# A four-layer graph network on one core: where a group's sums run, and when projections are issued

## The chip, the cores and the metric

The kernel runs on one core of a Trainium2 chip. The metric is the device time of one execution in microseconds (us); the time of a kernel is the median of its runs. Five engines with queues of their own work side by side: PE (matrix products; its weight loads are listed apart as PEld), DVE (vector), ACT (scalar functions), POOL, and SP, which here issues all large DMA transfers in the order of its queue.

## The reference, cut to what matters

There are N = 3327 nodes with D = 256 features, and a dense matrix `adj` of which about one per cent is not zero. Every layer normalizes, applies a ReLU and adds its result to x.

```python
# layer 0, two steps; R is adj + I with rows divided by their sums
for n in range(2):
    A = top_p_attention(Xa)          # softmax(q @ k.T); of each row, the largest
                                     # values that make up 0.9 of the sum are kept
    Xf = R @ Xf
    Xa = A @ Xa
    Z = Z + Xf @ U1[n].T + Xa @ U2[n].T
x = x + layernorm(h + Z)
# layer 1: weights tanh(adj * adj) where adj > 0
x = x + relu(new_adj @ (tanh(h @ W_proj + b_proj) @ W_gcn) + b_gcn)
# layers 2 and 3: graph attention over the places where adj > 0 (layer 2: or the diagonal)
Wh = h @ W
e = leaky_relu((Wh @ a[:256])[:, None] + (Wh @ a[256:])[None, :], 0.2)
x = x + softmax(where(mask, e, -9e15)) @ Wh      # layer 3: elu of this product
```

## The kernel before

The nodes are padded to 3328, 26 tiles of 128 rows. All products are in f32. The program is written tile by tile; a scheduler then orders the instructions of each engine when the kernel is built, so an engine's order is not quite that of the lines. During a run each engine goes through its own list in order.

**Layer 0.** In each of the two steps (s = 0 and 1) the rows are worked in groups of three tiles. For a group, scores are made (L1042) and moved from PSUM with a running maximum (L1016), exponentials are taken on ACT (L1025), and a threshold is sought for each row: a first guess (L1065 to L1104, with partial sums at L1085), and then four rounds (L1115 to L1158). A round sums, for each row, the values at or above the guess, and moves the guess. The sum of a tile is one pass on DVE (L1131), or two passes on ACT, a Relu and a Sign (L1126, written to `junk_a`), whose sums are put together on DVE (L1137, L1138). `ON_ACT = [2, 2, 1, 2]` says how many of a group's three tiles have their sums on ACT in each round. Before a round ACT negates the guess (`minus`, L1119); a round ends with a new guess (`v`, L1158). After the rounds the kept values are selected on DVE (L1173, L1176, L1187).

`weighted` then does a tile's attention product: transposes of the kept values (L951), their copy to `wt` on ACT (L953), 26 products (L941), the row `xa` (L963), a load of the tile's other row `xf_in` (L935), transposes of both (L785, copied at L786), and the product with U1 and U2 (L971).

`neighbours` makes one tile of R @ Xf: it loads the adjacency tile in four chunks `blk` (L906; three buffers), adds the diagonal on POOL (L913), runs 26 products into `ps_acc` (L915) and scales the row on ACT (`xf_row`, L923), which is written to memory (L924) and later read back as `xf_in`. In step 0 only, ACT also takes the sign of each chunk (`sg`, L909), and SP writes it out as int8 (`sign_d`, L910), to serve as the mask in layers 2 and 3. Groups overlap: a new one starts while the one before is in its products; during a group's rounds, `neighbours` of some tiles is laid beside it. The first group of a step has no earlier group's products beside it.

**Layer 1** is a loop over the 26 tiles (L1469 to L1500). Half a tile of `adj` is loaded (L1475), DVE multiplies (L1478), ACT takes the tanh (L1479), and PE runs 13 products (L1482) into `ps_wide`. Then `summed(it - 1)` adds bias and residual and takes statistics, and `entered2(it - 2)` prepares layer 2 for the tile two back: `Entry.tile_in` normalizes (`hr` on ACT, L1400), transposes (L785 on PE), copies to `ht` on ACT (L786), and projects on PE (L1405), with copies to `sd` and `wh` on ACT (L1409, L1410). After the last tile of each span of four, `spread` transposes and copies the column terms (L1422, L1425). The loop also loads rows of `adj` (L1494), from which DVE makes the mask `pos` (L1496).

**Layers 2 and 3** are `attention` over seven spans of four tiles: exponentials on ACT (L1585, L1586), their maximum and the mask on DVE (L1587, L1588), products on PE (L1594). While attention 2 runs, the finished tiles are prepared for layer 3 through the same `Entry`, in slots of a list `todo`. An `Entry` also makes, when it is created, a shift from its weights: a product on DVE, a matmul, a reduction and four small POOL steps (L1373 to L1385).

Of the kernel before, what the change touches and what calls it, by code (L numbers as in the profile page):

```python
# [20 lines left out]
P = 128  # L21
# [45 lines left out]
def kernel(  # L67
# [678 lines left out]
    def layers(fast):  # L746
# [54 lines left out]
        def layer0(wp, mp, ap_, tp, sp):  # L801
# [97 lines left out]
            def neighbours(s, it, xf):  # L899

                acc = ps_acc()
                w = XW if s == 0 else D
                for chunks in QB:
                    n = len(chunks)
                    blk = ap_.tile([P, 7, P], F32, tag="blk", name="blk")
                    nc.sync.dma_start(blk[:, :n, :], adj_t[it, :, chunks[0] : chunks[0] + n, :])  # L906
                    if s == 0:
                        sg = tp.tile([P, 7, P], I8, tag="sg", bufs=1, name="sg")
                        nc.scalar.activation(sg[:, :n, :], blk[:, :n, :], AF.Sign)  # L909
                        nc.sync.dma_start(sign_d[it, :, chunks[0] : chunks[0] + n, :], sg[:, :n, :])  # L910
                    if it in chunks:
                        j = it - chunks[0]
                        nc.gpsimd.tensor_tensor(blk[:, j, :], blk[:, j, :], ident, ALU.add)  # L913
                    for j, jc in enumerate(chunks):
                        nc.tensor.matmul(  # L915
                            acc[:, :w], blk[:, j, :], xf(jc)[:, :w], start=(jc == 0), stop=(jc == NT - 1)
                        )
                    yield
                yield
                if s == 0:  # L920
                    nc.vector.reciprocal(rr[:, it : it + 1], acc[:, D : D + 1])
                row = tp.tile([P, D], F32, tag="xf_row", name="xf_row")
                nc.scalar.mul(row, acc[:, :D], rr[:, it : it + 1])  # L923
                nc.sync.dma_start((xf_d, xf2_d)[s][it * P : (it + 1) * P, :], row)  # L924
                yield

            def weighted(s, it, e, norm, xa, xa_next, us):

                if s == 0:
                    base = h(it)[:, :D]  # L930
                else:
                    base = tp.tile([P, D], F32, tag="base", bufs=1, name="base_row")
                    nc.sync.dma_start(base, zz_d[it * P : (it + 1) * P, :])
                xf_in = tp.tile([P, D], F32, tag="xf_in", name="xf_in")
                nc.sync.dma_start(xf_in, (xf_d, xf2_d)[s][it * P : (it + 1) * P, :])  # L935
                po = ps_out0()[:, :D]

                def products(wt, j0, m):
                    for k in range(m):
                        jc = j0 + k  # L940
                        nc.tensor.matmul(  # L941
                            po, wt[:, k * P : (k + 1) * P], xa(jc)[:, :D], start=(jc == 0), stop=(jc == NT - 1)
                        )

                ready = None
                for j0 in range(0, NT, 8):
                    m = min(8, NT - j0)
                    pt = ps_wide()
                    for k in range(m):
                        jc = j0 + k  # L950
                        nc.tensor.transpose(pt[:, k * P : (k + 1) * P], e[:, jc * P : (jc + 1) * P], ident)  # L951
                    wt = tp.tile([P, 8 * P], F32, tag="wt", name="wt")
                    nc.scalar.copy(wt[:, : m * P], pt[:, : m * P])  # L953
                    if ready:
                        products(*ready)
                    ready = wt, j0, m
                    yield
                products(*ready)
                if s == 0:
                    row = xa_next(it)[:, :D]  # L960
                else:
                    row = tp.tile([P, D], F32, tag="xa_row", bufs=1, name="xa_row")
                nc.scalar.mul(row, po, norm)  # L963
                yield
                xt = turned(row, "xt", 2)
                xft = turned(xf_in, "xft", 2)
                yield
                pz = ps_row()
                for n, (lhs, u) in enumerate(((xft, us[0]), (xt, us[1]))):
                    for cc in range(2):  # L970
                        nc.tensor.matmul(  # L971
                            pz[:, :D], lhs[:, cc, :], u[:, cc, :],
                            start=(n == 0 and cc == 0), stop=(n == 1 and cc == 1),
                        )
                if s == 0:
                    keys_of(xt, 1, it)
                yield
                zrow = tp.tile([P, D], F32, tag="zrow", bufs=1, name="zrow")
                nc.vector.tensor_tensor(zrow, pz[:, :D], base, ALU.add)
                nc.sync.dma_start(zz_d[it * P : (it + 1) * P, :], zrow)  # L980
                if s == 1:
                    norm_of(zrow, sp, "mv_z", mv_z[:, it, :])
                yield
                if s == 0:

                    xb = tp.tile([P, D], F32, tag="xa_row", bufs=1, name="xb")
                    r = rows_of(it)
                    for a, b in rows_to_load(it):
                        nc.sync.dma_start(xb[a:b], x[it * P + a : it * P + b])
                    nc.gpsimd.tensor_tensor(xb[:r], xb[:r], b_b[:r], ALU.add)  # L990
                    nc.sync.dma_start(xb_d[it * P : it * P + r, :], xb[:r])
# [9 lines left out]
            def group(s, tiles, xa, xf, xa_next, us, slots, products_of, also):  # L1001
# [111 lines left out]
                todo = list(products_of)  # L1113
                first = 2 if g == len(todo) else 0
                for r in range(ROUNDS):  # L1115
                    on_act = list(range(max(g - ON_ACT[r], g - 2 if g > 2 else 1), g)) if g > 1 else []
                    A = slice(on_act[0], g) if on_act else None
                    if on_act:
                        nc.scalar.mul(minus[:, 0, A], v[:, 3, A], -1.0)  # L1119
# [239 lines left out]
        class Entry:  # L1359
# [3 lines left out]


            def __init__(self, name, w, wh, dk_tag, eye):
                self.w, self.wh, self.eye, self.mv = w, wh, eye, {}
                for t in wh.halves:
                    nc.gpsimd.memset(t[:, :, D : D + 1], 1.0)
                self.sd = late.tile([P, NT, 2], F32, name=f"sd{name}")
                self.d2 = late.tile([P, NT], F32, name=f"d2{name}")  # L1370
                self.dk = slot(dk_tag, [P, NP], f"dk{name}")
                self.tops = late.tile([P, 4, len(spans)], F32, name=f"tops{name}")
                sq = late.tile([P, 2], F32, tag="sq", name="sq")  # L1373
                nc.vector.tensor_tensor(sq, w[:, :, D + 1], w[:, :, D + 1], ALU.mult)
                ps = ps_row()
                nc.tensor.matmul(ps[:, :2], ones, sq, start=True, stop=True)
                self.shift = late.tile([P, 1], F32, name=f"shift{name}")
                self.low = late.tile([P, 1], F32, name=f"low{name}")
                shift = self.shift
                nc.vector.tensor_reduce(shift, ps[:, :2], AX.X, ALU.add)  # L1380
                nc.gpsimd.tensor_scalar(shift, shift, 1.01 * D, EPS, ALU.mult, ALU.add)
# [1 line left out]
                nc.gpsimd.tensor_scalar(shift, shift, 1.0, None, ALU.add)  # L1383

                nc.gpsimd.tensor_scalar(self.low, shift, -1.0 + 2.0**-20, None, ALU.mult)  # L1385
                if not eye:

                    self.part = late.tile([P, D + 1], F32, name="part")
                    nc.gpsimd.memset(self.part, 0.0)

            def stats(self, it, src):

# [1 line left out]
                nc.gpsimd.tensor_scalar(mv[:, 0:1], mv[:, 0:1], mv[:, 1:2], -1.0, ALU.mult, ALU.mult)  # L1394
                self.mv[it] = mv

            def tile_in(self, it, src):
                hr = late.tile([P, D], F32, tag="hr", bufs=2, name="hr")
                mv = self.mv.pop(it)
                nc.scalar.activation(hr, src, AF.Relu, bias=mv[:, 0:1], scale=mv[:, 1:2])  # L1400
                ht = late.tile([P, D], F32, tag="ht", bufs=2, name="ht")
                transposed(hr, ht)
                ps = ps_row()
                for c in range(2):
                    nc.tensor.matmul(  # L1405
# [47 lines left out]
        with tc.tile_pool(name="l1", bufs=2, reuse_waits="tile") as l1:  # L1453
# [7 lines left out]
                nc.vector.scalar_tensor_tensor(xn(it), pre, 0.0, xs(it), ALU.max, ALU.add)  # L1461
                entry2.stats(it, xn(it))

            def entered2(it):
                entry2.tile_in(it, xn(it))
                if it in ends:
                    entry2.spread(ends.index(it))

            for it in range(NT):  # L1469
# [15 lines left out]
                if it >= 1:  # L1485
                    summed(it - 1)
                if it >= 2:
                    entered2(it - 2)
                ar = slot(f"e{it % 2}", [P, NP], "adj_rows")
                r = rows_of(it)  # L1490
                if r < P:
# [7 lines left out]
                nc.gpsimd.memset(pos[:, N:], 0)  # L1499
                nc.sync.dma_start(pos_d[it], pos)  # L1500
            summed(NT - 1)
            entered2(NT - 2)
            entered2(NT - 1)


        att = fast.enter_context(tc.tile_pool(name="att", bufs=1, reuse_waits="tile"))
# [9 lines left out]
        def attention(entry, finish, following=None):  # L1516
# [33 lines left out]
            for i, span in enumerate(spans):  # L1550
# [16 lines left out]
                for b, j0 in enumerate(range(0, NT, JB)):  # L1567
# [30 lines left out]
                    if 1 <= b <= len(ahead):  # L1598
# [5 lines left out]
                        )  # L1604
                        if b == len(ahead):
                            sb_next = scores_of(ahead, top)
                    if b and todo:
                        for work in todo.pop(0):
                            work()
# [10 lines left out]
                if following is not None:  # L1620

                    stats = [lambda it=it: following.stats(it, xn(it)) for it in span]
                    rest = [lambda it=it: following.tile_in(it, xn(it)) for it in span]
                    todo += [stats[:2]] + [rest[k : k + 1] + stats[k + 2 : k + 3] for k in range(n)]
                    todo.append([lambda i=i: following.spread(i)])
            for works in todo:
                for work in works:
                    work()
# [106 lines left out]
```

## Time and profile before

| what | value |
|---|---|
| median of 3 runs | 3104.74 us (3103.69 to 3111.75) |
| the profiled execution | 3100.91 us, its span 3099.1 us |
| mean granted PE clock in it | 0.973 of full speed |
| step 0: first group's guess is made (L1104) | at 106.6 us |
| step 0: its rounds end (L1158) | at 132.8, 150.2, 160.1, 177.3 us |
| step 0: first L951 of groups 0 to 3 | at 197.2, 290.8, 386.5, 479.0 us |
| step 1: first group's guess, rounds' ends | at 1056.6; 1074.6, 1090.5, 1099.7, 1115.1 us |
| layer 1 | about 1999 to 2371 us |
| attention 2, attention 3 | about 2371 to 2765, and to the end |

A line of the costliest groups names a line, an engine, an operation and output <- inputs; then the number of instructions, their busy time and the mean ns of one, and the idle time of the engine just ahead of them with what ended most of it. A line of the waits says which instruction waited for which, how many us in all, how often, and the longest. A line of the timeline gives start and length of an instruction, and in brackets the idle time before it.

### The profile page before, as it was taken

The page shows a single profiled execution, that of the slowest core. Times are in us where ns is not written, and L with a number is a line of the kernel's source. Part 1 is how long each engine was busy: PE and PEld are TensorE (multiplying, and loading weights), DVE is VectorE, ACT ScalarE, POOL GpSimd, SP SyncE. Part 2 cuts the span into 40 slices and gives each one's busy share as a digit, 9 for nine tenths or more (in the row PEclk, how much of TensorE's full clock was granted, in tenths as well). Part 3 has the DMA queues.
Part 4 walks back from the last instruction along what each step waited for, and adds up shares of the span by engine and source line. Part 5 has one row for each costly group of instructions (what it writes and reads, how often), then busy time and mean ns, then how long its engine had stood idle before and what let it go on. Part 6 is the DMA issues. An engine that isn't in the chain of part 4 may idle for free.

```text
span 3099.1 us, 37681 instructions
## 1 busy us (share of the span) xinstructions
PE 2823.0 (91%) x13454; PEld 2277.8 (73%) x13454; DVE 2370.4 (76%) x4133; ACT 1979.7 (64%) x2633; POOL 417.8 (13%) x742
## 2 busy tenths in 40 slices
PE   7788899999999899999999988999997999979998
PEld 5466677777778576667777767888886887758887
DVE  3678889778874588889876858377765999769996
ACT  6767787768773566687666555433334777657776
POOL 0120010000001001111110024211110333210000
PEclk9889999999999999999999989999998999989999
DMA  4431112321242231211232231388871211112221
GB/s 138 131 102 45 55 45 76 95 78 57 75 121 87 73 103 53 64 35 54 74 90 72 83 114 60 105 321 318 324 243 32 71 59 59 30 48 78 75 74 37
DMA packets 183035, 298.83 MB, mean 96 GB/s; under 512 B 24701, under 2 KB 137016, under 8 KB 179512
## 3 DMA queue, kind: packets, MB, share of 16 engines
q1 hardware_dynamic: 182838, 296.34, 30.3%
q8 instruction: 108, 1.77, 0.3%
q14 instruction: 89, 0.72, 0.1%
HBM read 251.97 MB, written 44.30 MB: 96 GB/s over the span
## 4 chain that ended last, share of the span: by engine, by line
DVE 38%; PE 27%; ACT 16%; issue 8%; DMA 7%; POOL 3%; SPq 0%; ACTq 0%; POOLq 0%; DVEq 0%
ACT junk_a L1126 9%; PE ps_wide L1594 5%; DVE below L1173 4%; PE ps_out L941 4%; PE ps_acc L915 4%; DVE w L1176 4%; PE ps_wide L1482 4%; DVE below L1131 3%; DVE e L1187 3%; DVE places L1601 3%; DVE places L1587 2%; DVE below L1085 2%; DVE places L1588 2%; DMA blk<-in_adj_t 2%; DMA adj_rows<-in_adj 2%
## 5 line engine op out<-in xcount | busy, mean ns | idle before, releaser
L1126 ACT ACTIVATE junk_a<-e,minus 128x3328 int8<-128x3328 f32 x208 | 638.8, 3071 | 3.7
L1594 PE MATMUL ps_wide<-wh,places 128*128 128x257 f32 x1872 | 451.2, 383 | 35.6 <-DVE places L1588 32.7
L1594 PEld LDWEIGHTS ps_wide<-wh,places 128*128 128x128 f32 x1872 | 353.3, 191 | 93.6 <-ACT places L1586 16.5
L915 PE MATMUL ps_acc<-h,blk 128*128 128x258 f32 x1352 | 333.3, 399 | 46.8 <-ACT xf_row L923 37.1
L915 PEld LDWEIGHTS ps_acc<-h,blk 128*128 128x128 f32 x1352 | 261.8, 198 | 102.3 <-ACT xf_row L923 42.7
L1016 DVE TENSOR_SCALAR_CACHE_REDUCE e<-ps_wide 128x1024 f32<-128x1024 f32 (+1 forms) x176 | 178.6, 1019 | 206.9 <-PE ps_wide L1042 206.4
L915 PE MATMUL ps_acc<-xf,blk 128*128 128x256 f32 x1352 | 312.9, 384 | 14.3 <-ACT xf_row L923 14.2
L941 PE MATMUL ps_out<-h,wt 128*128 128x256 f32 x1352 | 311.2, 381 | 4.7 <-ACT wt L953 4.7
L941 PE MATMUL ps_out<-xa,wt 128*128 128x256 f32 x1352 | 311.9, 381 | 0.9 <-ACT wt L953 0.7
L1585 ACT ACTIVATE places<-places,sd 128x512 f32<-128x512 f32 (+1 forms) x364 | 246.3, 684 | 100.5 <-PE ps_wide L1594 67.6
L1482 PE MATMUL ps_wide<-gw,blk 128*128 128x256 f32 x1352 | 300.9, 379 | 1.3 <-ACT blk L1479 1.3
L915 PEld LDWEIGHTS ps_acc<-xf,blk 128*128 128x128 f32 x1352 | 253.9, 191 | 61.8 <-ACT xf_row L923 19.3
L1482 PEld LDWEIGHTS ps_wide<-gw,blk 128*128 128x128 f32 x1352 | 254.5, 190 | 35.0 <-ACT blk L1479 1.7
L941 PEld LDWEIGHTS ps_out<-h,wt 128*128 128x128 f32 x1352 | 249.8, 190 | 40.1 <-ACT wt L953 6.3
L941 PEld LDWEIGHTS ps_out<-xa,wt 128*128 128x128 f32 x1352 | 249.4, 190 | 34.8 <-ACT wt L953 3.0
L1586 ACT ACTIVATE places<-places,d 128x512 f32<-128x512 f32 (+1 forms) x364 | 235.8, 682 | 48.7 <-DVE places L1587 48.2
L1131 DVE SCALAR_TENSOR_TENSOR below<-e,v 128x3328 f32<-128x3328 f32 x72 | 265.3, 3684 | 1.8
L1587 DVE TENSOR_TENSOR places<-places,places 128x1024 f32<-128x1024 f32 (+1 forms) x182 | 210.2, 1163 | 65.8 <-ACT places L1585 63.7
L1042 PE MATMUL ps_wide<-keys,q 64*128 64x512 f32 (+1 forms) x832 | 215.9, 570 | 17.8 <-DVE e L1016 14.8
L953 ACT COPY wt<-ps_wide 128x1024 f32<-128x1024 f32 x208 | 175.2, 846 | 86.2 <-PE ps_wide L951 85.6
L1588 DVE SCALAR_TENSOR_TENSOR places<-blk_s,places 128x1024 f32<-128x1024 int8 (+1 forms) x182 | 206.3, 1142 | 2.0
L1176 DVE MAX8 w<-below 128x8 f32<-128x3328 f32 x52 | 188.3, 3621 | 0.3
(275 smaller groups left out, 4312.6 us busy)
## 6 DMA issues: line engine op xcount, KB each, us to landing
blk<-in_adj_t SPq DMA_DIRECT2D x104, 448.0 KB, 3.5
blk<-in_adj_t SPq DMA_DIRECT2D x52, 832.0 KB, 7.1
adj_rows<-in_adj SPq DMA_DIRECT2D x25, 1663.5 KB, 8.4
blk<-in_adj_t SPq DMA_DIRECT2D x104, 384.0 KB, 3.3
blk_s<-sign_d SPq DMA_DIRECT2D x72, 256.0 KB, 2.9
blk_s<-pos_d SPq DMA_DIRECT2D x44, 416.0 KB, 3.6
pos_d<-pos SPq DMA_DIRECT2D x22, 416.0 KB, 2.9
xf_d<-xf_row SPq DMA_DIRECT2D x52, 128.0 KB, 2.4
```

The lines of the kernel that those rows point to most:

```text
L915: nc.tensor.matmul(acc[:, :w], blk[:, j, :], xf(jc)[:, :w], start=(jc == 0), stop=(jc == NT - 1))
L941: nc.tensor.matmul(po, wt[:, k * P : (k + 1) * P], xa(jc)[:, :D], start=(jc == 0), stop=(jc == NT - 1))
L1042: nc.tensor.matmul(pl[:, f * 512 : f * 512 + cw], q[f * DA : (f + 1) * DA, :], kt[f * DA : (f + 1) * DA, s, c0 : c0 + cw], start=True, sto ...
L1126: nc.scalar.activation(junk, es[i], (AF.Relu, AF.Sign)[n], bias=minus[:, 0, i : i + 1], accum_out=(ga, sa)[n][:, 0, i : i + 1],)
L1131: nc.vector.scalar_tensor_tensor(below, es[i], v[:, 3, i : i + 1], es[i], ALU.is_ge, ALU.mult, accum_out=v[:, 1, i : i + 1],)
L1176: nc.vector.max(w9[:, i, 1:9], below)
L1482: nc.tensor.matmul(po, filt[:, j * P : (j + 1) * P], gw(jc), start=(jc == 0), stop=(jc == NT - 1))
L1585: nc.scalar.activation(e1[:, :, q, :], s0, AF.Exp, bias=sd[:, jc + q, 1:2])
L1586: nc.scalar.activation(e2[:, :, q, :], s1, AF.Exp, bias=d2[:, jc + q : jc + q + 1])
L1587: nc.vector.tensor_tensor(e1, e1, e2, ALU.max)
L1588: nc.vector.scalar_tensor_tensor(e1, signs[:, :n, j : j + 2, :], 0.0, e1, ALU.is_gt, ALU.min)
L1594: nc.tensor.matmul(pos_[k], e1[:, k, q, :], wh(jc + q)[:, : D + 1], start=(jc + q == 0), stop=(eye and jc + q == NT - 1),)
```

## The change

It has four parts.

- In `neighbours`, `sg` gets the pool's two buffers in place of one; in `weighted`, `xf_in` gets one in place of two.
- In the rounds, the group that holds tile 0 has `most = 1`, so only its last tile has its sums on ACT in every round; all others keep `ON_ACT`. This is the first group of step 0 and of step 1.
- `tile_in` is split into `turned` (normalize, transposes, copy to `ht`) and `projected` (products, copies). In layer 1's loop, pass `it` does `turned(it - 2)` and `projected(it - 3)`; in attention 2's list, a slot has `turned` of one tile and `projected` of the tile before.
- The shift is made by a function `shifted`, called in the loop's pass 2 for layer 2, and in the second span of attention 2 for layer 3, rather than when the `Entry` is created.

```diff
-                        sg = tp.tile([P, 7, P], I8, tag="sg", bufs=1, name="sg")
+                        sg = tp.tile([P, 7, P], I8, tag="sg", name="sg")
...
-                xf_in = tp.tile([P, D], F32, tag="xf_in", name="xf_in")
+                xf_in = tp.tile([P, D], F32, tag="xf_in", bufs=1, name="xf_in")
...
-                    on_act = list(range(max(g - ON_ACT[r], g - 2 if g > 2 else 1), g)) if g > 1 else []
+
+                    most = 1 if tiles[0] == 0 else ON_ACT[r]
+                    on_act = list(range(max(g - most, g - 2 if g > 2 else 1), g)) if g > 1 else []
...
-            def tile_in(self, it, src):
+            def turned(self, it, src):
                 hr = late.tile([P, D], F32, tag="hr", bufs=2, name="hr")
                 mv = self.mv.pop(it)
                 nc.scalar.activation(hr, src, AF.Relu, bias=mv[:, 0:1], scale=mv[:, 1:2])
-                ht = late.tile([P, D], F32, tag="ht", bufs=2, name="ht")
-                transposed(hr, ht)
+                self.ht[it] = late.tile([P, D], F32, tag="ht", bufs=2, name="ht")
+                transposed(hr, self.ht[it])
+
+            def projected(self, it):
+                ht = self.ht.pop(it)
                 ps = ps_row()
...
                 if it >= 2:
-                    entered2(it - 2)
+                    entry2.turned(it - 2, xn(it - 2))
+                if it == 2:
+                    entry2.shifted()
+                if it >= 3:
+                    projected(it - 3)
...
             summed(NT - 1)
-            entered2(NT - 2)
-            entered2(NT - 1)
+            projected(NT - 3)
+            entry2.turned(NT - 2, xn(NT - 2))
+            projected(NT - 2)
+            entry2.turned(NT - 1, xn(NT - 1))
+            projected(NT - 1)
...
+                    if following is not None and (i, b) == (1, 1):
+                        following.shifted()
...
-                    rest = [lambda it=it: following.tile_in(it, xn(it)) for it in span]
-                    todo += [stats[:2]] + [rest[k : k + 1] + stats[k + 2 : k + 3] for k in range(n)]
-                    todo.append([lambda i=i: following.spread(i)])
+                    turned = [lambda it=it: following.turned(it, xn(it)) for it in span]
+                    made = [lambda it=it: following.projected(it) for it in span]
+                    todo += [stats[:2]] + [
+                        turned[k : k + 1] + made[max(k - 1, 0) : k] + stats[k + 2 : k + 3] for k in range(n)
+                    ]
+                    todo.append(made[-1:] + [lambda i=i: following.spread(i)])
```

The rest of the diff moves the shift's lines unchanged from `__init__` into `shifted`.

More of the change, by code (lines that the diff above doesn't have):

```diff
@@ L1365, in __init__ @@
             def __init__(self, name, w, wh, dk_tag, eye):
-                self.w, self.wh, self.eye, self.mv = w, wh, eye, {}
+                self.w, self.wh, self.eye, self.mv, self.ht = w, wh, eye, {}, {}
                 for t in wh.halves:
@@ L1372, in __init__, with shifted @@
                 self.tops = late.tile([P, 4, len(spans)], F32, name=f"tops{name}")
+                self.shift = late.tile([P, 1], F32, name=f"shift{name}")
+                self.low = late.tile([P, 1], F32, name=f"low{name}")
+                if not eye:
+                    self.part = late.tile([P, D + 1], F32, name="part")
+                    nc.gpsimd.memset(self.part, 0.0)
+            def shifted(self):
                 sq = late.tile([P, 2], F32, tag="sq", name="sq")
-                nc.vector.tensor_tensor(sq, w[:, :, D + 1], w[:, :, D + 1], ALU.mult)
+                nc.vector.tensor_tensor(sq, self.w[:, :, D + 1], self.w[:, :, D + 1], ALU.mult)
                 ps = ps_row()
                 nc.tensor.matmul(ps[:, :2], ones, sq, start=True, stop=True)
-                self.shift = late.tile([P, 1], F32, name=f"shift{name}")
-                self.low = late.tile([P, 1], F32, name=f"low{name}")
                 shift = self.shift
@@ L1385, in __init__ @@
                 nc.gpsimd.tensor_scalar(self.low, shift, -1.0 + 2.0**-20, None, ALU.mult)
-                if not eye:
-                    self.part = late.tile([P, D + 1], F32, name="part")
-                    nc.gpsimd.memset(self.part, 0.0)
             def stats(self, it, src):
@@ L1462, in summed, with projected @@
                 entry2.stats(it, xn(it))
-            def entered2(it):
-                entry2.tile_in(it, xn(it))
+            def projected(it):
+                entry2.projected(it)
                 if it in ends:
```

## The prediction

> **What bounds the kernel now.** I read the page's busy shares and costliest groups first, then busy time by stage, then the waits of PE, DVE and ACT in the stages that the change touches, and last the timeline of one of them.
>
> ```profile
> PE 2823.0 (91%) x13454; PEld 2277.8 (73%) x13454; DVE 2370.4 (76%) x4133; ACT 1979.7 (64%) x2633; POOL 417.8 (13%) x742
> L1126 ACT ACTIVATE junk_a<-e,minus 128x3328 int8<-128x3328 f32 x208 | 638.8, 3071 | 3.7
> L915 PE MATMUL ps_acc<-h,blk 128*128 128x258 f32 x1352 | 333.3, 399 | 46.8 <-ACT xf_row L923 37.1
> L1131 DVE SCALAR_TENSOR_TENSOR below<-e,v 128x3328 f32<-128x3328 f32 x72 | 265.3, 3684 | 1.8
> ```
>
> PE is busy for 91%, so over the whole kernel a gain must be PE idle time taken away: 276 us of the 3099.1 us span. Where that idle time lies is seen by stage. The columns are the stretch, its length, busy PE, PEld, DVE, ACT and POOL, granted clock, DMA share, GB/s.
>
> ```profile
> 110.00:197.00 87.00, 62.02 (x232) 49.28 (x233) 49.23 (x109) 64.73 (x58) 26.81 (x27) 0.82 0.51 150
> 197.00:291.00 94.00, 80.24 (x388) 61.25 (x387) 76.93 (x147) 72.15 (x75) 4.31 (x18) 0.95 0.17 48
> 291.00:386.00 95.00, 85.67 (x414) 65.33 (x413) 82.67 (x161) 71.99 (x75) 2.55 (x16) 0.96 0.17 48
> 386.00:479.00 93.00, 87.26 (x438) 67.33 (x437) 75.94 (x140) 72.92 (x78) 9.54 (x17) 1.00 0.20 59
> 1056.00:1133.00 77.00, 68.14 (x295) 54.98 (x296) 49.77 (x111) 53.30 (x42) 7.91 (x14) 0.96 0.48 133
> 2010.00:2343.00 333.00, 319.85 (x1507) 276.19 (x1506) 226.87 (x265) 111.86 (x154) 53.24 (x109) 1.00 0.79 288
> 2371.00:2736.00 365.00, 339.79 (x1564) 286.60 (x1563) 321.48 (x437) 253.44 (x471) 113.38 (x105) 0.99 0.19 57
> ```
>
> The first row is where step 0's first group searches its threshold with nothing but `neighbours` products to lay beside it. PE idles 25.0 us there, DVE 37.8, ACT 22.3: no engine is full, so a chain sets the pace. The next three rows, groups 1 to 3, are nearer to PE (13.8, 9.3 and 5.7 us idle). The fifth is step 1's first group, the sixth layer 1's loop, the last attention 2. In the first row PE, DVE and ACT wait so:
>
> ```profile
> PE ps_acc L915 <- ACT xf_row L923: 17.6, 5, 8.3
> DVE sa L1137 <- ACT junk_a L1126: 13.1, 2, 10.8
> ACT sg L909 <- DMA sign_d<-sg: 18.3, 6, 5.4
> ```
>
> DVE, done with its one tile's sum, waits for ACT's two tiles:
>
> ```profile
> 133.02 3.69 DVE L1131 SCALAR_TENSOR_TENSOR below<-e,v 128x3328 f32<-128x3328 f32 x1
> ...
> 148.08 0.16 DVE L1137 SCALAR_TENSOR_TENSOR sa<-sa,v 128x2 f32<-128x2 f32 x1 [10.77 <-ACT junk_a L1126]
> ```
>
> And in layer 1's loop PE waits for the copy of the tile that it has just transposed, once in about every second tile:
>
> ```profile
> PE ps_row L1405 <- ACT ht L786: 11.1, 11, 2.6
> ```
>
> **What the Trainium skill says.** "TensorE: Matmul & The Clock Gate", Part 1, says that ScalarE and VectorE run strictly in order. The trace agrees: `xf_row` (0.46 us) stands behind the 3.06 us `junk_a` passes while PE waits 8.3 us for it, and the copy `ht` behind a tanh. The same Part 1 says that an idle window of some 3.4 us halves PE's clock; with the PE gaps of up to 8.3 us in the first row goes a granted clock of 0.82, against 0.96 to 1.00 in full stages, so idle time removed there is repaid a little more than once. "Perfetto Trace Analysis", Optimization Strategy, says that a gap that repeats can mean too few buffers: ACT's waits for `sign_d` to leave the single `sg` fit that (54.9 us over step 0).
>
> **The first group of step 0 (one tile's sums on ACT).** The four rounds end (L1158) at 132.8, 150.2, 160.1 and 177.3, after a start at 106.6 (L1104): 26.2, 17.4, 9.9 and 17.2 us. The third already has one tile on ACT; the others have two. Removed on ACT: 14 passes become 8, so 6 x (3.06 + 0.19) = 19.5 us. Added on DVE: 3 x (3.68 + 0.08) = 11.3 us, in its 37.8 us of idle time. A round with two sums on DVE is 2 x 3.76 + about 2.4 of small steps = 9.9, as the third shows. Round 1 keeps two exponentials of group 1 (6.5 us) and four `sg`; I take 15, then 12.5, 9 and 9.5: 46, ending at 152.5 rather than 177.3. The chain is 24.7 us shorter.
>
> Not all of that is time. The order in which the changed kernel issues work to PE has 130 `neighbours` products ahead of the first weighted transposes (L951) instead of 164. The 34 left out take 11.2/26 = 0.43 us each by the stretches of 26, so 14.6 us, and come later: the counts ahead of groups 1 and 2 are 156 against 191 and 208 against 234, and equal from group 3. From there the order is the same, so the gain is just the PE idle time that goes away before 479. If none of the returned products finds a gap, it is 24.7 - 14.6 = 10.1; if they filled all of 14.6 out of the 28.8 us of gaps in groups 1 to 3 it would be the whole 24.7; if all gaps move there it is nothing, since PE's wait for `xf_row` also stands in those groups (11.7 us). DVE carries 76.9 and 82.7 us there and ACT 72, so little is free. I take -10 (0 to -25).
>
> **Two `sg`, one `xf_in`.** In the first row ACT waits 18.3 us for `sign_d`; of this the wait that in turn holds PE is what the second buffer gains. After the passes are thinned some 5 us of PE's `xf_row` wait remain, and I take -3 (0 to -8). One `xf_in` makes each of the 52 loads (L935) wait on SP for the transposes of the tile just before, with adjacency loads queued behind. A load takes 2.0 us to land, and it is read some 26 products later. In the changed order of SP the next adjacency loads stand ahead of it. I take 0 (0 to +5).
>
> **The first group of step 1.** Rounds of 18.0, 15.9, 9.1 and 15.4 us (1056.6 to 1115.1) become about 11, 10.5, 9 and 10, so 58.4 becomes 41: -17.5. 30 `neighbours` products (811 against 841 ahead of its first L951) come back, 12.9 us. Net -5; PE's idle time of 8.9 us in this row bounds the gain (+2 to -9).
>
> **Layer 1.** PE gets the transposes of tile `it-2` and then the projection of `it-3`, side by side; before, only two products, 1.03 us, lay between a tile's transposes and its own projection. The 11.1 us of waits go: a whole tile, 12.3 us, now covers the copy. Work is the same; ht's two buffers hold both live tiles. Nothing is added to SP. Then DMA is next: its share, 0.79 over the loop, rises by 3%. SP's loads wait for PE (`ps_wide`, 109.7 us), not the other way round, so I take -10 (0 to -11). The shift sum (L1374 to L1385: one DVE step, one matmul, one reduction, four on POOL) moves from the end into the loop. It costs nothing there: POOL is busy for 53 of 333 us; before, DVE waited 8.0 us for it at the end, but `dk` came only 0.1 us later, so removing it brings 0.
>
> **Attention 2 and the ends.** The same wait is 5.7 us over attention 2 with its end; the work hangs in slots beside mask products, and PE also waits for DVE's masks (8.4 us), which can take its place. -2 (+2 to -6). At the two ends (28 us with PE busy 10.6, 29 with 13.3) both transposes now go first and projections follow, hiding one copy: -1 in sum (+1 to -3).
>
> **Sum:** -10 - 3 + 0 - 5 - 10 - 2 - 1 = -31 on the profiled execution's 3100.9 us, so 3070. The median stands 3.8 us above that execution, so 3074.
>
> **Rivals.**
> 1. *The first groups give everything back.* Their 27.5 us of returned products meet full engines, and the wait for `xf_row` moves to groups 1 and 2. For: the products return before group 3. Against: groups 1 to 3 have 28.8 us of PE gaps. Left are -10 - 2 - 1, so 3092.
> 2. *Layer 1 has another limit.* The row loads and `pos` (DVE waits 40.0 us for `adj_rows`) or the adjacency stream set the loop, and the removed waits reappear on L1482. For: DMA share 0.88 in its steady slices. Against: PE waits for `blk` only 1.3 us in 333. Then -18 - 3, so 3084.
> 3. *Slower: SP's queue jams on the single `xf_in`.* SP waits for transposes before L935 already 28 times, 152.7 us. If each of 52 loads now holds the next adjacency load by 1 us more than PE has in hand, that is +52 - 31, so 3126. It decides from about 0.8 us a load (40 us over 52: the 31 gained and 9 to be seen). Against: in the first groups, PE waits for `blk` 0.9 us in all, and three `blk` buffers are in hand.
> 4. *DVE becomes the bound of the first group*: its `rr` (L921) stands in line before sums and waits for PE (15.3 us in the first row). With two sums a round on DVE the chain gains 12, not 25, less than the products moved out; step 0's first group then costs +3, the whole 3087.
>
> **Numbers.** A measurement of this kernel tells about 0.3%, 9.3 us, from no change. Forecast 0.60, rivals 0.13, 0.10, 0.10 and 0.07. From the forecast's own spread (the ends above, taken together as independent, about 16 us either way) its range is 3056 to 3092. Rivals 1, 2 and 4 lie within or at its upper edge; reaching to 3104 takes their tails in and leaves out the slower case, and down to 3048 takes in the full 24.7 us. Faster 0.80 (nearly all of the forecast, two thirds of rival 1, nearly all of 2 and 4), same 0.10, slower 0.10.
>
> **What would show it.** First rounds all near 10 to 15 us, no wait of 10 us at L1137, first L951 near 172; ACT's `sign_d` waits cut; the third group's start 10 to 15 us earlier; no wait of the projection for `ht` and a loop of about 323 us in layer 1; the stretch of attention 2 nearly unchanged. It would be wrong if groups 1 to 3 get longer by what group 0 saves, if L1482 starts to wait for `blk`, or if SP's wait ahead of the `xf_in` loads lets PE wait for `blk` at L915.

## The result and the profile after

The changed kernel takes 3090.59 us (median of 6 runs, 3087.34 to 3094.6) against 3104.77 us of the kernel before (6 runs, 3101.63 to 3111.75): ratio 0.9949, 95% interval 0.9938 to 0.996, so 14.2 us less. The forecast was 31 us less, 3074 us. The measured time lies at the upper end of the forecast's own spread (3056 to 3092) and nearest to rival 1's 3092, so the number alone does not tell the forecast from its rivals. The profiled execution took 3091.2 us, its span 3089.4 us.

The page of the changed kernel, the lines that answer to the ones shown of the kernel before (in the new file `junk_a` is L1128, the sum on DVE L1133, a round's new guess L1160):

```profile
PE 2825.1 (91%) x13454; PEld 2287.0 (74%) x13454; DVE 2394.1 (77%) x4145; ACT 1942.3 (63%) x2609; POOL 399.6 (13%) x742
L1128 ACT ACTIVATE junk_a<-e,minus 128x3328 int8<-128x3328 f32 x196 | 602.0, 3071 | 4.1
L915 PE MATMUL ps_acc<-h,blk 128*128 128x258 f32 x1352 | 331.7, 398 | 44.1 <-ACT xf_row L923 35.8
L1133 DVE SCALAR_TENSOR_TENSOR below<-e,v 128x3328 f32<-128x3328 f32 x78 | 287.7, 3689 | 1.9
```

Twelve passes went from ACT and six came to DVE, as counted. But PE's wait for `xf_row` in step 0, the largest one forecast to shrink, is 35.8 us after 37.1. Busy time by stage in the changed kernel (columns as before: stretch, length, PE, PEld, DVE, ACT, POOL, clock, DMA share, GB/s): the first group of step 0, the first of step 1, layer 1's loop, attention 2.

```profile
110.00:180.00 70.00, 49.63 (x172) 37.16 (x173) 59.11 (x109) 41.71 (x37) 26.04 (x22) 0.79 0.44 131
1048.00:1114.00 66.00, 58.79 (x256) 46.06 (x255) 64.54 (x126) 36.98 (x31) 8.24 (x15) 0.97 0.46 126
2001.00:2334.00 333.00, 321.39 (x1520) 280.29 (x1518) 229.59 (x273) 111.72 (x157) 42.94 (x112) 0.99 0.78 288
2360.00:2726.00 366.00, 340.04 (x1565) 289.33 (x1564) 322.32 (x437) 251.56 (x470) 111.45 (x109) 0.98 0.19 57
```

The first two rows, which end about where the first group's products (L951) begin, are 17 and 11 us shorter than their counterparts. The rows of the loop and of attention 2 are only cut at about the same length as before; from its first product to its last, layer 1 takes 341.2 us after 344.5, where 10 us less were forecast. In the first row PE still idles 20.4 of 70 us, and the granted clock is 0.79 after 0.82, so the prediction's hope that idle time removed there is repaid more than once doesn't show. What the engines wait for in that row:

```profile
PE ps_acc L915 <- ACT xf_row L923: 18.0, 3, 6.8
PE ps_acc L915 <- DMA blk<-in_adj_t: 7.4, 2, 4.0
...
DVE sa L1139 <- ACT junk_a L1128: 3.3, 1, 3.3
...
ACT sg L909 <- DMA blk<-in_adj_t: 23.6, 6, 11.9
ACT sg L909 <- DMA sign_d<-sg: 1.7, 1, 1.7
...
SPq L991 <- POOL xb L990: 24.9, 9, 5.2
```

DVE's long wait for ACT is gone and so is ACT's for `sign_d`. In its place ACT and PE wait for adjacency blocks. SP, which issues their loads, waits for POOL, as it did before (29.5 us in the 87 us of that row). The timeline of the second round on DVE, start and length in us, shows that two sums now run one after the other and ACT's one is done in time:

```profile
125.63 3.69 DVE L1133 SCALAR_TENSOR_TENSOR below<-e,v 128x3328 f32<-128x3328 f32 x1
...
129.65 3.67 DVE L1133 SCALAR_TENSOR_TENSOR below<-e,v 128x3328 f32<-128x3328 f32 x1
...
135.12 0.15 DVE L1139 SCALAR_TENSOR_TENSOR sa<-sa,v 128x1 f32<-128x1 f32 x1
```

The lead of a kernel over the profiled execution of before, read from the same instructions in both traces, says where the time went (us; negative is earlier):

```
                                  changed   sums_step0  projections  spread_xb
step 0: first group's rounds end    -18.0      -23.3        -2.1       -30.1
step 0: last xa of group 1          -17.3      -21.2        -2.5       -32.0
step 0: last xa of group 2          -10.7      -12.5        -2.5       -19.9
step 0: last xa of group 4           -3.6       -6.5        -0.8       -17.0
step 0: its last xa                  -2.1       -6.4        -1.6        -9.6
step 1: first group's rounds end    -18.8       -6.7        -1.6       -26.3
step 1: last xa_row of group 3       -7.5       -6.4        -1.8       -15.3
step 1: its last xa_row              -8.4       -7.1        -3.4       -16.7
layer 1: its last product           -11.6       -4.6        -6.9       -25.9
attention 2: its last row            -8.9       -3.5        -4.1       -23.1
```

In both steps the first group gains 16 to 18 us and groups 1 to 4 lose most of it again. The profiled execution of before was 3.9 us quicker than the median of its runs, so a gain by time can be larger than these leads, and in step 0 a few us are within what one and the same program varies (last section).

### The profile page after: what moved, and what is told of

Same layout as the page of the kernel before. It is cut to its first block, busy times and chain, and to the rows that moved or that the text cites. A ratio compares the mean times of both kernels' runs of the same rounds, so it can differ in the third digit from the quotient of the medians.

```text
span 3089.4 us, 37720 instructions
## 1 busy us (share of the span) xinstructions
PE 2825.1 (91%) x13454; PEld 2287.0 (74%) x13454; DVE 2394.1 (77%) x4145; ACT 1942.3 (63%) x2609; POOL 399.6 (13%) x742
## 4 chain that ended last, share of the span: by engine, by line
DVE 29%; PE 26%; ACT 9%; issue 7%; DMA 5%; POOL 2%; SPq 1%; ACTq 0%; DVEq 0%; POOLq 0%
PE ps_wide L1608 6%; ACT junk_a L1128 5%; PE ps_out L941 5%; PE ps_acc L915 3%; DMA adj_rows<-in_adj 3%; DVE below L1133 3%; DVE places L1615 3%; PE ps_wide L1489 3%; DVE w L1178 3%; DVE below L1175 3%; DVE places L1601 2%; DVE places L1602 2%; DVE below L1085 2%; DVE e L1189 2%; DMA blk<-in_adj_t 2%
## 5 line engine op out<-in xcount | busy, mean ns | idle before, releaser
L1128 ACT ACTIVATE junk_a<-e,minus 128x3328 int8<-128x3328 f32 x196 | 602.0, 3071 | 4.1
L915 PE MATMUL ps_acc<-h,blk 128*128 128x258 f32 x1352 | 331.7, 398 | 44.1 <-ACT xf_row L923 35.8
L1133 DVE SCALAR_TENSOR_TENSOR below<-e,v 128x3328 f32<-128x3328 f32 x78 | 287.7, 3689 | 1.9
```

Source lines behind the costliest of these rows:

```text
L915: nc.tensor.matmul(acc[:, :w], blk[:, j, :], xf(jc)[:, :w], start=(jc == 0), stop=(jc == NT - 1))
L1128: nc.scalar.activation(junk, es[i], (AF.Relu, AF.Sign)[n], bias=minus[:, 0, i : i + 1], accum_out=(ga, sa)[n][:, 0, i : i + 1],)
L1133: nc.vector.scalar_tensor_tensor(below, es[i], v[:, 3, i : i + 1], es[i], ALU.is_ge, ALU.mult, accum_out=v[:, 1, i : i + 1],)
```

## The experiments

Ratios are to the kernel before on the same chip, with 95% intervals; 0.001 is 3.1 us.

**Step 0's first group alone** is the kernel before with

```diff
-                    on_act = list(range(max(g - ON_ACT[r], g - 2 if g > 2 else 1), g)) if g > 1 else []
+                    most = 1 if tiles[0] == 0 and s == 0 else ON_ACT[r]
+                    on_act = list(range(max(g - most, g - 2 if g > 2 else 1), g)) if g > 1 else []
```

> The kernel before with one change: the first group of step 0 alone has one tile's sums on ACT. Theory (the shorter search is given back inside step 0, since its neighbours products only come later): the first L951 some 17 us earlier, but step 0 ends within 3 us of before; ratio 0.999 to 1.001. Rival (the prediction's size): 10 us kept, ratio 0.9967.

Measured: 0.9979 (0.9968 to 0.999), about 6.5 us. At the end of group 0 the lead is 21.9 us, and all but one of the 34 `neighbours` products put off are still to come; at group 4 it is 6.5. The 15.4 us lost are near what 33 products take at 0.43 us each, 14.2, so on balance they found no gap. It isn't even: ten of them come back in group 1 for 0.7 us, and the other 23, some 10 us of work, in groups 2 to 4 for 14.7. What is left is about the chain's gain less those products, as the prediction had it, but smaller than its 10; neither end of what was expected here fits exactly.

**Step 1's first group alone**: the same edit with `s == 1`.

> The kernel before with one change: the first group of step 1 alone has one tile's sums on ACT. Theory: -18 us at the end of the first group, -5 us at the end of step 1 and of the kernel; ratio 0.998 to 0.9985. Rival: given back in full as in step 0, ratio 1.000.

Measured: 0.999 (0.9983 to 0.9998), 3 us. In its trace step 1 is 5.8 us shorter than before's. Over all traces, from the last `xa` of step 0 to the last `xa_row`, it takes 980.4 to 982.2 us in the five kernels looked at with two sums on ACT, and 974.8 to 976.4 in the nine with one. The theory holds in its working; the timed gain is at the small end.

**The buffers alone**: the kernel before with

```diff
-                        sg = tp.tile([P, 7, P], I8, tag="sg", bufs=1, name="sg")
+                        sg = tp.tile([P, 7, P], I8, tag="sg", name="sg")
...
-                xf_in = tp.tile([P, D], F32, tag="xf_in", name="xf_in")
+                xf_in = tp.tile([P, D], F32, tag="xf_in", bufs=1, name="xf_in")
```

> The kernel before with one change: two sg buffers and one xf_in buffer. Theory: ACT's wait for sign_d goes, but the adjacency loads are held by the queue of SP, so nothing changes: ratio 0.9995 to 1.0005. Rival (the prediction's size): -3 us, ratio 0.999. Rival (SP jams on xf_in): above 1.003.

Measured: 1.000 (0.9991 to 1.0009). Neither the 3 us of the prediction nor the slower rival. In the trace ACT's waits for `sign_d` in the first group are gone, and 18.5 us of waits for `blk` stand there instead.

**The projections alone**: the changed kernel with these two parts undone.

```diff
-                    most = 1 if tiles[0] == 0 else ON_ACT[r]
+                    most = ON_ACT[r]
...
-                        sg = tp.tile([P, 7, P], I8, tag="sg", name="sg")
+                        sg = tp.tile([P, 7, P], I8, tag="sg", bufs=1, name="sg")
...
-                xf_in = tp.tile([P, D], F32, tag="xf_in", bufs=1, name="xf_in")
+                xf_in = tp.tile([P, D], F32, tag="xf_in", name="xf_in")
```

> The changed kernel with the sums and the buffers as before, so that only the split of tile_in and the moved shift stay. Theory: PE's wait for ht in layer 1 (12.8 us) goes, and a wait of the spread for sd of some 10 us takes its place, so layer 1 gains 1 us, and 2.5 at its end; ratio 0.9985 to 0.9995. Rival (the prediction's size): -13 us, ratio 0.9958.

Measured: 0.9968 (0.9955 to 0.998), some 10 us, 6 to 14. That is more than the theory gave and near the prediction. The trace doesn't show as much. The span is 5.8 us shorter than before's: 3.5 in layer 1 (341.0 us from its first to its last product, 344.5 before), 3.4 ahead of it, which this edit doesn't touch, and nothing gained behind it. That before's profiled execution was 3.9 us quicker than its median explains a part of the difference; where the rest of the timed gain lies wasn't found.

**The changed kernel with the buffers as before**, to see what they cost beside the new sums (the last two edits of the diff above, alone).

> The changed kernel with one sg and two xf_in buffers, as before. Theory (the second sg only turns ACT's wait for sign_d into one for blk, and SP's order delays the adjacency loads): the first group of step 0 ends 4 us earlier than in the changed kernel and this stays; ratio to before 0.993 to 0.9945. Rival (buffers are worth nothing or a little): ratio as the changed kernel's, 0.995 or above.

Measured: 0.9957 (0.9943 to 0.997), no faster than the changed kernel's 0.9949. In the profiled execution step 0 ended 6.5 us earlier than in the changed kernel's, but that execution (3081.11 us) was the quickest of its five, whose median is 3089.33. The theory fell by time. One thing in the traces is clear: here and in the run of step 0's sums alone PE waits for no block in the first group, and ACT waits for `sign_d` again (15.2 and 11.2 us). In the changed kernel it is the other way round. What the buffers cost or bring in time beside the new sums is less than these runs tell.

**xb out of SP's way.** The queue of SP in the changed kernel during the first group (start, length, what is issued) shows what the adjacency loads stand behind:

```profile
142.92 0.33 SPq L989 DMA_DIRECT2D xb<-in_x  x1
145.91 0.32 SPq L991 DMA_DIRECT2D xb_d<-xb  x1
146.28 0.42 SPq L906 DMA_DIRECT2D blk<-in_adj_t  x1
147.62 0.33 SPq L989 DMA_DIRECT2D xb<-in_x  x1
148.05 0.38 SPq L906 DMA_DIRECT2D blk<-in_adj_t  x1
```

`weighted` ends with a piece that the prediction didn't look at: it loads the tile's x as `xb`, adds a bias on POOL and stores it. It needs nothing else, so the scheduler puts it early, one after the other through one buffer: all 26 adds have started by 204 us. Each store (L991) waits for its add, and the block load behind it waits too: the load issued at 146.28 ends PE's wait of 3.39 us at 149.66. The edit gives `xb` the buffer of `zrow`, so that a tile's `xb` comes when its own `zrow` is through. The adds then start between 203 and 1012 us:

```diff
-                    xb = tp.tile([P, D], F32, tag="xa_row", bufs=1, name="xb")
+                    xb = tp.tile([P, D], F32, tag="zrow", bufs=1, name="xb")
```

> The changed kernel with xb (the load, add and store of x plus a bias for each tile) in the buffer of zrow, so that each waits for its own tile's end instead of all standing early in SP's queue. Theory (in step 0's first group SP waits some 30 us for POOL's xb adds with adjacency loads behind): PE's 7.4 us of waits for blk there go, step 0 ends 4 to 7 us earlier; ratio 0.993. Rival (SP isn't in the way): 0.995, and the same waits stand at other names.

Measured: 0.9948 (0.9935 to 0.9962) by time, which can't be told from the changed kernel. The waits of its first group did change as the theory says:

```profile
PE ps_acc L915 <- ACT xf_row L923: 10.6, 4, 4.8
PE ps_wide L1042 <- DVE e L1016: 6.5, 2, 3.7
...
SPq L906 <- PE ps_acc L915: 21.7, 11, 5.5
SPq L910 <- ACT sg L909: 18.5, 9, 7.7
```

PE waits for no block any more, SP waits for PE and ACT instead of POOL, and the group's rounds end at 147.4 us, 12 earlier than in the changed kernel. Its five runs lie between 3077.51 and 3091.53 us, too far apart to price it; the pair below does.

**The spread one tile later.** In layer 1 the changed kernel's PE has another wait in the place of the one for `ht`:

```profile
PE ps_row L1429 <- ACT sd L1416: 10.3, 5, 2.9
```

Its timeline on PE at one such place:

```profile
2134.70 0.38 PE L785 MATMUL ps_row<-ident,hr 128*128 128x128 f32 x2
2134.92 1.04 PE L1412 MATMUL ps_row<-w2l,ht 128*128 128x258 f32 x4
2138.87 0.65 PE L1429 MATMUL ps_row<-ident,sd 128*128 128x128 f32 x4 [2.92 <-ACT sd L1416]
```

After the last projection of a span (L1412) its `spread` (L1429) follows at once. It transposes `sd`, which ACT must first copy from that projection; here two tanh (L1486) run on ACT from 2135.50 us for 3.05 us, and `sd` is copied at 2138.72. The edit puts a tile between them:

```diff
-            def projected(it):
-                entry2.projected(it)
+            def spread(it):
                 if it in ends:
                     entry2.spread(ends.index(it))
...
                 if it >= 3:
-                    projected(it - 3)
+                    entry2.projected(it - 3)
+                if it >= 4:
+                    spread(it - 4)
```

The last tiles follow suit after the loop.

> The changed kernel with each spread in layer 1 issued one tile later than the projection that it reads. Theory: PE's 10.3 us of waits for sd (L1416) go, layer 1 takes 8 us less; ratio 0.9925. Rival (loads of adjacency tiles and rows limit the loop, and waits come back on L1489's blk): ratio 0.995.

Measured: 0.995 (0.9936 to 0.9964), nothing gained, though not for the rival's reason: PE waits 1.7 us for blocks, and for `ht` at the spread.

```profile
PE ps_row L1429 <- ACT ht L786: 8.8, 3, 3.7
PE ps_wide L1488 <- ACT blk L1485: 1.7, 1, 1.7
```

The spread reads no `ht`. Its timeline, on PE and on ACT:

```profile
2100.06 0.38 PE L785 MATMUL ps_row<-ident,hr 128*128 128x128 f32 x2
2100.28 1.04 PE L1412 MATMUL ps_row<-w2l,ht 128*128 128x258 f32 x4
2104.99 1.11 PE L1429 MATMUL ps_row<-ident,sd 128*128 128x128 f32 x4 [3.67 <-ACT ht L786]
```

```profile
2101.27 1.59 ACT L1485 ACTIVATE blk<-blk 128x1664 f32<-128x1664 f32 x1 [7.68 <-DVE blk L1484]
2103.07 1.59 ACT L1485 ACTIVATE blk<-blk 128x1664 f32<-128x1664 f32 x1 [0.21 <-DVE blk L1484]
2104.57 0.36 ACT L786 ACTIVATE ht<-ps_row 128x256 f32<-128x256 f32 x1
```

All three kinds of PE work write `ps_row`, which has two banks. The transposes took one, the projection the other, and the spread needs the first again. That is free when the copy `ht` has emptied it, and the copy stands behind two tanh.

**The spread in another bank.** late_spread with

```diff
+        spread_acc = [True]
+
         def ps_spread():
-            return ps_row()
+            return ps_acc() if spread_acc[0] else ps_row()
```

and the flag cleared after layer 1, where `ps_acc` has no other use in the steady loop. The changed kernel itself ran beside it, and two further versions.

> The changed kernel itself, beside the next ones on one chip: ratio 0.995, as measured.

> The kernel late_spread with layer 1's spreads in the ps_acc bank in place of one of the two ps_row banks. Theory (after the move the spread still waited 8.8 us, for the ps_row bank that the copy ht must empty): PE waits for neither sd nor ht there, and from the first to the last product of layer 1 it takes 6 to 10 us less than in the changed kernel; ratio 0.992 to 0.993. Rival (the adjacency and row loads limit the loop): the stretch stays within 2 us and waits for blk grow at L1488.

Measured: the changed kernel 0.9953 (0.9939 to 0.9966), spread_acc 0.9929 (0.9915 to 0.9942). In layer 1 the waits are down to

```profile
PE ps_row L785 <- ACT hr L1404: 6.8, 3, 3.4
PE ps_row L1412 <- ACT ht L786: 1.4, 2, 1.2
PE ps_wide L1490 <- ACT blk L1487: 0.9, 1, 0.9
```

and the steady loop to

```profile
2001.00:2326.00 325.00, 320.02 (x1515) 279.58 (x1514) 229.55 (x273) 110.65 (x158) 45.33 (x112) 0.99 0.79 295
```

with 5.0 us of idle PE and about the same DMA share (0.79 after 0.78). The waits above are those up to 2334 us, which takes in the loop's end; up to 2326 us the wait for `hr` is 3.4 us and none for `ht` is left. From the first product to the last, layer 1 takes 345.2 us on average in the five kernels with the old entry (342.7 to 346.9), 341.6 in the six with the split alone or with the late spread (339.6 to 343.7), and 334.4 in the three with the other bank (333.4 to 335.3). The ranges of the first two groups overlap, the third stands clear of both. The loads weren't what had held the loop at its old length.

**Both mends**: spread_acc with `xb` in the buffer of `zrow`, and the same with one `sg` and two `xf_in`.

> spread_acc with xb in the buffer of zrow as well. Theory: SP's stall in step 0's first group goes too, another 10 us; ratio 0.989 to 0.991. Rival (that lead is given back): the ratio of spread_acc.

> spread_xb with one sg and two xf_in buffers, as in the kernel before. Theory (with SP free of xb, the second sg is no longer paid for by late loads, so the buffers are worth about 2 us): ratio within 0.001 of spread_xb, on its slow side. Rival (one xf_in costs): 0.001 to 0.002 below it.

Measured: 0.9894 (0.9878 to 0.9909), 3073.97 us median, and 0.9911 (0.9897 to 0.9924), 3080.28 us. The first is better than spread_acc with intervals apart, so `xb` was worth some 11 us of time there. The buffers come out at 0.0017, with intervals that overlap, so they can't be told from nothing. spread_xb beats both kernels of this study: 17 us less than the changed kernel on the same chip. Its page shows PE at a higher share:

```profile
PE 2818.5 (92%) x13454; PEld 2284.6 (74%) x13454; DVE 2393.1 (78%) x4145; ACT 1940.3 (63%) x2609; POOL 401.9 (13%) x742
```

**xb alone**: the kernel before with that one edit.

> The kernel before with xb in the buffer of zrow and nothing else. Theory (SP's stall counts only once ACT's two sums a round no longer set the first group's pace): first group ends within 4 us of before, ratio 0.998 to 1.000. Rival (the stall holds the first group whatever ACT does): 10 us, ratio 0.9968.

Measured: 1.0001 (0.9993 to 1.001). The first group ends 8.6 us earlier, more than the theory allowed: SP's stall did hold that group in the kernel before as well. The lead is not lost beside the first group either. It is 11.0 us at group 1 and still 10.5 at group 3; it goes in groups 4 to 7, and step 0 ends 1.0 us later than before. There the `xb` pieces now stand, and between 685 and 1019 us SP waits 27.6 us for their adds; in the kernel before it waited for none there. So the edit moves the stall, and pays for it where it lands; that this wait is what eats the lead is likely but was not tried. The kernels with `xb` moved and the new sums lose less there, 5 to 8 us from group 4 to the end of step 0, and keep some of their lead.

## Why the prediction was right in its direction and half in its size

**The first group of step 0.** The mechanism was right, and the chain of the rounds was sized well: 24.7 us shorter was said, 23.3 came in the run of this part alone. That the products come back was right as well. "I take -10" became -6.5 (-10 to -3) by time. In the changed kernel as a whole the trace keeps only 2 us of it. There the rounds took 17.6, 11.7, 10.0 and 12.5 us in place of 15, 12.5, 9 and 9.5 (the last two lie below the 9.9 that the prediction itself had for such a round), and ended at 159.3 in place of 152.5. What failed, by the traces, is that the sums and the buffers were added up as if neither touched the other. "PE waits for `blk` 0.9 us in all" was read from the kernel before. With the new sums alone, or the buffers alone, it stays near that (0 and 0.4 us); with both it is 7.4 us (6.1 to 7.4 in the four traces that have both), behind the stores of `xb`. With `xb` where it was, step 0 ends at 1013.8 to 1021.0 us in the four traces with the new sums and two `sg`, and at 1010.4 and 1008.2 in the two with the new sums and one. By time that loss was not shown.

**Two `sg`, one `xf_in`.** "I take -3" was wrong: nothing, alone. ACT's 18.3 us of waits for `sign_d` did go, to 1.7, but came back as waits for `blk`: 23.6 us, and 18.5 with the buffers alone. "Some 5 us of PE's `xf_row` wait remain" failed too: 18.0 us remain of 17.6. A buffer for the signs helps only if the next block has come, and its load stood in SP's queue. The slower rival, the jam on the single `xf_in`, didn't occur. SP did hold up block loads, as that rival had it, but at `xb`, and it did so in the kernel before too.

**The first group of step 1.** "Net -5": 5.7 us in the traces and 3 (0.6 to 5) by time. Right, with the same working; there are no `xb` pieces in step 1, and in its first group neither PE nor ACT waits for a block.

**Layer 1.** "The 11.1 us of waits go", with "a loop of about 323 us", is the step that failed in layer 1. The waits for `ht` went, down to nothing in the changed kernel's steady loop, but 10.3 us of waits of the spread came. The working followed transposes and projection and named what hides them, and it never followed the spread, the next reader of a projection, nor the two banks that all three share. On average of the traces the split is worth 3.6 us there, and 10.8 once the spread has a bank of its own and a tile of distance. So in the traces -10 was the right size for a different edit. By time the split with the moved shift came to 10 us without that edit, which the traces don't account for; so the step is shown wrong by the waits and the length of the loop, not by the time of this part. Rival 2, that DMA or DVE limits the loop, is refuted as what kept the loop long: that run shortened it under the same loads.

**Attention 2 and the ends.** -3 was said. From layer 1's last product to the last row of attention 2 the changed kernel takes 391.2 us against 388.5. PE's 8.0 us of waits for `ht` there fell to 1.5, and waits for `sd` (3.3 us), `col` (7.8 after 6.6) and masks (32.6 after 30.5) grew. The prediction had named masks as what could take its place; its upper end, +2 there and +1 at the ends, was nearer than its value. This is one pair of traces, and no run changed this part alone.

**The sum.** By time the parts alone give -6.5, 0, -3 and -10, together 19.5, where -10, -3, -5 and -13 were said; the whole change is 14 to 16 (12 to 19). In the pair of traces the change is short of its terms by 11 us in step 0 (2 of 13), by 7 in layer 1 (3 of 10) and by some 5 behind it, and 1 us ahead in step 1. So most of what is missing there lies in two steps of the prediction, the adding up of two parts in step 0 and the spread that it left out in layer 1; attention 2 stays open. The moved shift was not tried by itself. Rival 1, that the first groups give everything back, is nearly true of step 0 inside the whole change, where the lead of 17.3 us at group 1 is 3.6 at group 4, and untrue of each group's sums alone. Rival 4, DVE as the bound of step 0's first group, said that the chain would gain 12 us; it gained 18 to 23, with DVE busy for 59.1 of 70 us.

## What to carry to other kernels

When a wait on a copy is hidden by moving its reader back, follow the next reader too, and every user of the PSUM banks between them: with two banks and three users in a row, the wait on the copy came back here under another line, 8.8 us of it. When a chain is shortened by moving work away from it, price the work at its full length where it lands, unless a gap there is named. Parts that use the same queue are not added up as if they were alone. And a queue that issues loads in order is read for what stands in front of the loads: work with no inputs of its own was placed early by the scheduler here, where it held the loads, and moved to a later place it made the queue wait there (27.6 us).

## What the runs showed that was not expected

Step 0 varies from one execution to another. Four profiled kernels have the same instructions in the same order in its first group (the changed kernel twice, late_spread and spread_acc); its rounds ended at 159.3, 156.7, 164.7 and 155.6 us, and step 0 at 1014.7, 1014.7, 1021.0 and 1013.8. Three others have step 0 as in the kernel before (that kernel, the projections alone and step 1's sums alone), and there it ended at 1016.8, 1015.3 and 1021.2. Step 1 hardly varies: with the same sums it takes 974.8 to 976.4 us in every trace. Layer 1 lies between, 342.7 to 346.9 us in the five kernels with the old entry. So differences of up to 6 us in step 0 or 4 in layer 1 can't be read from two traces; they take many runs, or several traces on each side.
